# Four-layer vision kernel: dt·u·B moved to TensorE as a product with diagonal matrices, C·h to GpSimd, the scan as a pipeline of two-state units

## Chip, cores and metric

One core of one Trainium2 chip. The time is the device time of one execution in microseconds; the three runs of the kernel before have a median of 46869.22 us. All arithmetic is fp32.

## What is computed

x is [4 images, 64 x 64 pixels, 192 channels]. Four layers, each `x = x + layer(groupnorm(x))`:

- Layers 0 and 3 (state space scans over an image): project x to u (384 channels in layer 0, 192 in layer 3), depthwise 3x3 convolution and silu. Then the 4096 pixels are one sequence, taken in four orders: by rows, by columns, and both backwards. The four results are added, normalised, gated and projected back.
- Layer 1: the same kind of scan, with each image row (and each image column) as a sequence of its own of 64 pixels, forwards and backwards: four blocks with 384 channels, each with its own projections and a convolution of four taps.
- Layer 2: Toeplitz products along rows and columns. The change doesn't touch it.

The scan at the heart of layers 0, 1 and 3, for each channel and each of 16 states n:

```python
dA = jnp.exp(dt_l[..., None] * A[None])
h = dA * h + (dt_l * u_l)[..., None] * Bl[:, :, None, :]
y = jnp.sum(h * Cl[:, :, None, :], axis=-1)
```

dt has a value per channel and pixel (a softplus of a projection of rank 12); B and C have 16 values per pixel, the same for all channels. D·u is added to y.

## The kernel before

Channels lie on partitions, in NT tiles of P: 3 of 128 in layers 0 and 1, 2 of 96 in layer 3. Pixels run along the free dimension. A **job** is one chunk of 512 pixels of one image in one order: 4 images x 4 orders x 8 chunks = 128 jobs in each of the three layers.

`prepare` (line 101) makes the steps of a job: one projection of u gives 44 rows, the rank-12 part of dt, B and C (line 111). B and C go to DRAM (line 115). Per tile a second matmul and ScalarE and VectorE instructions make delta and dtu = delta·u (lines 121 to 139).

`scan` (line 143) is one job's loop over n = 0..15. For two states at a time, B and C are loaded from DRAM, broadcast over the partitions (line 159, 1 MB, 0.75 MB in layer 3). Then for each n:

1. VectorE: h = dtu·B, one product over all NT tiles (line 161, [P, NT x 512]); it is issued for n + 1 before the product with C for n.
2. ScalarE: dA = exp(A·delta), one instruction a tile (line 179 in layer 1, line 188 otherwise).
3. VectorE: the scan h = dA·h + h. In layers 0 and 3 one instruction a tile (line 191), which starts from `carry`, the state at the end of the previous chunk, which ScalarE copies out (line 194). In layer 1 one instruction over all tiles (line 184): dA holds zeros where a sequence begins.
4. VectorE: hc = h·C (line 198).
5. TensorE: y += I·hc, one matmul a tile that adds up in PSUM over n (line 200); y begins with D·u, a matmul with a diagonal matrix (line 172).

`run_jobs` (line 90) writes the order out by hand: the steps after the last job (layer 1: gate and output projection; layers 0 and 3: `add` of y to `acc`, line 311) and those that prepare the next job are spread evenly between the sixteen n of a scan. Each engine runs its own queue in that order; all DMAs are issued from SyncE's queue (SP).

In layers 0 and 3, `ss2d_input` leaves u in SBUF; a job in column order reads it through a strided view (`view`, line 300). PSUM: two one-bank buffers `mm` for projections, and two of three banks for y.

Of the kernel before, what the change touches and what calls it, by code (L numbers as in the profile page):

```python
# [7 lines left out]
F32 = mybir.dt.float32  # L8
# [5 lines left out]
B, HW, L = 4, 64, 4096  # images, their side, pixels of one  # L14
C = 192  # channels of the residual stream, as two tiles of 96 partitions
PC, KC = 96, 2
N = 16  # states per channel
R = 12  # rank of the step sizes
E = R + 2 * N
T = 512  # pixels of one chunk  # L20
NCH = L // T
ROWS = T // HW  # image rows (or columns) of one chunk
NG = 2  # states per load of the broadcast B and C
D1, PD, KD = 576, 96, 6  # channels of the Toeplitz layer, as six tiles of 96


class Kernel:
    def __init__(self, ctx, tc, ins, out):
        self.tc, self.nc, self.i, self.out = tc, tc.nc, ins, out
        nc = self.nc  # L30
        self.const = ctx.enter_context(tc.tile_pool(name="const", bufs=1))
        self.dram = ctx.enter_context(tc.tile_pool(name="dram", bufs=1, space=DRAM))
        self.bcd = ctx.enter_context(tc.tile_pool(name="bcd", bufs=4, space=DRAM))
        self.ident = self.const.tile([128, 128], F32, name="ident")
        make_identity(nc, self.ident)
        self.group = self.const.tile([PC, PC], F32, name="group")
        nc.sync.dma_start(self.group, ins["c_group"])
        # Turns each half of the partitions round.
        self.flip = self.const.tile([128, 128], F32, name="flip")
        nc.sync.dma_start(self.flip, ins["c_flip"])  # L40
        self.eps = self.const.tile([128, 1], F32, name="eps")
        nc.vector.memset(self.eps, 1e-5)
# [41 lines left out]
    # A job is one chunk: P, NT channel partitions and tiles; u(), its inputs [P, NT, T] or  # L84
    # [P, NT, ROWS, HW]; w, the weights; rev, whether it runs backwards; first, whether its state
    # starts at 0; carry, the state between chunks by n (None: each image row or column is a
    # sequence of its own, and dA holds tiles that are 0 where one begins); before, steps that
    # make u; after(y), steps that use the chunk's y, its D u included, from PSUM.

    def run_jobs(self, jobs, pools):  # L90
        """The steps before the next chunk and after the last one go between those of a scan."""
        for step in self.prepare(jobs[0], pools):
            step()
        after = []
        for job, following in zip(jobs, jobs[1:] + [None]):
            between = after + (self.prepare(following, pools) if following else [])
            after = job["after"](self.scan(job, pools, between))
        for step in after:
            step()

    def prepare(self, job, pools):
        """Steps to delta, delta u, and B and C in DRAM."""
# [4 lines left out]
        def project():  # L107
            u = job["u"]()
# [5 lines left out]
            job["bc"] = self.bcd.tile([2, N, T], F32, name="bc_dram")  # L114
            nc.sync.dma_start(job["bc"].rearrange("a n l -> (a n) l"), xd[R:E, :])
            job["delta"] = prep.tile([P, NT, T], F32, name="delta")
            job["dtu"] = prep.tile([P, NT, T], F32, name="dtu")
            job["e"] = prep.tile([P, NT, T], F32, name="e", bufs=1)

        # softplus(v) = max(v, 0) + log1p(exp(-|v|)), log1p(e) = ln(q) + (e - (q - 1)), q = 1 + e  # L120
        def step_size(t):
            dp = mm.tile([P, T], F32, name="dt_ps", tag="mm")
            nc.tensor.matmul(dp, w["dtw"][:, t * P : (t + 1) * P], job["xd"][0:R, :], start=True, stop=True)  # L123
# [10 lines left out]
        def finish():  # L134
            e, delta, dtu, u = job["e"], job["delta"], job["dtu"], job["u"]()
            nc.vector.tensor_sub(delta, delta, e)  # L136
            nc.vector.tensor_add(delta, delta, dtu)  # L137
            by_line = lambda ap: ap.rearrange("p t (a b) -> p t a b", b=HW) if len(u.shape) == 4 else ap
            nc.vector.tensor_mul(by_line(dtu), by_line(delta), u)

        return job["before"] + [project] + [lambda t=t: step_size(t) for t in range(NT)] + [log1p, finish]

    def scan(self, job, pools, between):
        nc = self.nc
        P, NT, w, rev, carry = (job[k] for k in ("P", "NT", "w", "rev", "carry"))
        delta, dtu, scratch, u = job["delta"], job["dtu"], job["bc"], job["u"]()
        work = pools["work"]
        lines = lambda ap: ap.rearrange("p (a b) -> p a b", b=HW)
        flat = lambda ap: ap.rearrange("p t l -> p (t l)")
        way = slice(None, None, -1) if rev else slice(None)  # L150
        inner = slice(0, HW - 1) if rev else slice(1, HW)
        last = 0 if rev else T - 1
        bc = {}

        def state_input(n):
            if n % NG == 0:
                bc[n // NG] = pools["bc"].tile([P, 2, NG * T], F32, name="bc")
                src = scratch[:, n : n + NG, :].rearrange("a n l -> a (n l)")
                nc.sync.dma_start(bc[n // NG], src.unsqueeze(0).broadcast_to([P, 2, NG * T]))
            h = work.tile([P, NT, T], F32, name="h")  # L160
            nc.vector.tensor_mul(h, dtu, spread(n, 0))  # L161
            return h

        def spread(n, which):
            at = (n % NG) * T
            return bc[n // NG][:, which, at : at + T].unsqueeze(1).broadcast_to([P, NT, T])

        if job.get("begin"):
            job["begin"]()
        y = pools["y"].tile([P, NT, T], F32, name="y")  # L170
        for t in range(NT):
            nc.tensor.matmul(y[:, t, :], w["D"][:, t, :], u[:, t], start=True, stop=False)  # L172
        h_next = state_input(0)
        for n in range(N):
            h = h_next
            if carry is None:
                dA = job["dA"][n % len(job["dA"])]
                for t in range(NT):
                    nc.scalar.activation(  # L179
                        lines(dA[:, t, :])[:, :, inner], lines(delta[:, t, :])[:, :, inner],  # L180
                        AF.Exp, scale=w["A"][:, t, n : n + 1],
                    )
                h_way = flat(h)[:, way]
                nc.vector.tensor_tensor_scan(h_way, flat(dA)[:, way], h_way, 0.0, ALU.mult, ALU.add)  # L184
            else:
                dA = work.tile([P, NT, T], F32, name="dA")
                for t in range(NT):
                    nc.scalar.activation(dA[:, t, :], delta[:, t, :], AF.Exp, scale=w["A"][:, t, n : n + 1])  # L188
                for t in range(NT):
                    start = 0.0 if job["first"] else carry[n][:, t : t + 1]  # L190
                    nc.vector.tensor_tensor_scan(  # L191
                        h[:, t, way], dA[:, t, way], h[:, t, way], start, ALU.mult, ALU.add
                    )
                nc.scalar.copy(carry[n], h[:, :, last])  # L194
            if n + 1 < N:
                h_next = state_input(n + 1)
            hc = work.tile([P, NT, T], F32, name="hc")
            nc.vector.tensor_mul(hc, h, spread(n, 1))  # L198
            for t in range(NT):
                nc.tensor.matmul(y[:, t, :], self.ident[:P, :P], hc[:, t, :], start=False, stop=n == N - 1)  # L200
            for step in between[len(between) * n // N : len(between) * (n + 1) // N]:
                step()
        return y

    def neg_exp(self, A):
        """A_log -> -exp(A_log), in place."""
# [4 lines left out]
    def ss2d(self, pre, x_in, x_out, P, NT, ways, bias_twice):  # L211
        tc, nc, ins = self.tc, self.nc, self.i
        DI = P * NT
        xn_d = self.image_tiles(f"{pre}xn")
        with tc.tile_pool(name=f"{pre}lay", bufs=1) as lay:
# [5 lines left out]
            D = self.load(lay, "D", ins[f"{pre}D"])  # L221
            dtb = self.load(lay, "dtb", ins[f"{pre}dt_b"])
# [7 lines left out]
            u = lay.tile([P, NT, L], F32, name="u")  # L230
            acc = lay.tile([P, NT, L], F32, name="acc")
            for b in range(B):
                self.ss2d_input(x_in[b], xn_d[b], u, P, NT, inw, cw, cb)
                self.ss2d_scan(pre, u, acc, P, NT, ways, A, D, dtb)
                self.ss2d_output(x_in[b], xn_d[b], x_out[b], acc, P, NT, inw, ow, g, be, avg)

    def ss2d_input(self, x_in, xn_d, u, P, NT, inw, cw, cb):
        """Group norm, input projection, depthwise 3x3 convolution, silu -> u."""
        tc, nc = self.tc, self.nc
        S = HW + 2  # L240
        with (
            tc.tile_pool(name="a", bufs=1) as pa,
            tc.tile_pool(name="a_small", bufs=1) as small,
# [583 lines left out]
```

## Time and profile before

| | |
|---|---|
| Runs | 46856.47, 46869.22, 46886.22 us |
| Profiled execution, span | 46860.2 us |
| Mean granted TensorE clock | 0.761 |
| DMA | 3594.65 MB, mean 77 GB/s |
| Layer 0, jobs of one image (204 to 4046 us) | 3842 us for 32 jobs |
| Layer 1, all jobs (16955 to 31620 us) | 14665 us for 128 jobs |

The profiled execution is one execution; its span runs from the first to the last instruction. In lines of groups, columns are: line of the kernel, engine, operation, tiles written and read, shapes, count, then busy time in us, mean ns of one, and idle time of the engine before them with what ended it. PE is TensorE (PEld its weight loads), DVE is VectorE, ACT ScalarE, POOL GpSimd.

### The profile page before, as it was taken

Reading aid. Unit: us, or ns where it says so; the run is one execution under the profiler, and the core shown is the slowest. Engines: PE = TensorE matmul, PEld = TensorE weight load, DVE = VectorE, ACT = ScalarE, POOL = GpSimd, SP = SyncE. Lnnn points to the kernel's source line nnn. Section 1 sums busy time; section 2 is a strip of 40 time slices with the busy share of each in tenths; the row PEclk is TensorE's granted clock in tenths of the full one; section 3 lists DMA queues with packets and bytes.
Section 4 is the critical chain, followed back from the end, with each engine's and each line's share of the span. In section 5 each row is a group of like instructions: output and inputs, shape, how many; then the busy total and the mean of one; then the engine's idle time right before and its main releaser. Section 6 shows DMA issues by size and latency. Waiting matters only on the chain. (4 is left out here: it accounts for less than half of the span.)

```text
span 46860.2 us, 220354 instructions
## 1 busy us (share of the span) xinstructions
PE 34545.4 (74%) x67176; PEld 12468.0 (27%) x67176; DVE 42630.1 (91%) x28512; ACT 18863.3 (40%) x29431; POOL 96.4 (0%) x30
## 2 busy tenths in 40 slices
PE   6666666666666667777777777777887877878778
PEld 2222222222222223333333333332652222222222
DVE  9999999899999989999999999992226999999999
ACT  3333333333333335555555555550323333333333
POOL 0000000000000000000000000000000000000000
PEclk7777777777777788888888888887997555565555
DMA  2221222222222232222222222224333222222222
GB/s 67 71 70 65 70 71 70 65 70 70 65 71 70 70 97 80 80 81 81 80 81 80 80 81 80 80 79 103 70 84 85 80 75 80 78 77 79 76 80 78
DMA packets 1162895, 3594.65 MB, mean 77 GB/s; under 512 B 229685, under 2 KB 234374, under 8 KB 1153638
## 3 DMA queue, kind: packets, MB, share of 16 engines
q1 hardware_dynamic: 1161702, 3580.55, 25.1%
q8 instruction: 528, 8.65, 0.1%
q14 instruction: 665, 5.45, 0.0%
HBM read 3353.17 MB, written 227.08 MB: 76 GB/s over the span
## 5 line engine op out<-in xcount | busy, mean ns | idle before, releaser
L200 PE MATMUL y<-hc,ident 128*128 128x512 f32 (+1 forms) x32768 | 22752.0, 854 | 9493.5 <-DVE hc L198 9492.8
L200 PEld LDWEIGHTS y<-hc,ident 128*128 128x128 f32 (+1 forms) x32768 | 7791.3, 253 | 24490.0 <-DVE hc L198 14676.2
L191 DVE TENSOR_TENSOR_SCAN h<-dA,carry,h 128x512 f32<-128x512 f32 (+1 forms) x8960 | 10904.3, 1268 | 0.0
L198 DVE TENSOR_TENSOR hc<-h,bc 128x1536 f32<-128x1536 f32 (+1 forms) x6144 | 9562.3, 1570 | 17.0 <-PE y L200 2.1
L161 DVE TENSOR_TENSOR h<-dtu,bc 128x1536 f32<-128x1536 f32 (+1 forms) x6144 | 9502.4, 1565 | 7.6 <-ACT carry L194 1.1
L194 ACT COPY carry<-h 128x3 f32<-128x3 f32 (+1 forms) x4096 | 794.2, 194 | 15450.3 <-DVE h L191 15450.2
L184 DVE TENSOR_TENSOR_SCAN h<-dA,h 128x1536 f32<-128x1536 f32 x2048 | 6757.3, 3341 | 0.0
L188 ACT ACTIVATE dA<-delta,A 128x512 f32<-128x512 f32 (+1 forms) x10240 | 6691.0, 711 | 3.1
L179 ACT ACTIVATE dA<-delta,A 128x504 f32<-128x504 f32 x6144 | 3959.4, 706 | 4961.1 <-DVE h L184 4672.5
L172 PE MATMUL y<-u,Dd 128*128 128x512 f32 (+1 forms) x2048 | 1281.5, 750 | 628.8 <-issue 601.8
L191 DVE TENSOR_TENSOR_SCAN h<-dA,h 128x512 f32<-128x512 f32 (+1 forms) x1280 | 1479.7, 1206 | 0.0
L501 PE MATMUL conv_ps<-pad,taps 128*128 128x512 f32 x3072 | 1381.8, 591 | 0.0
L132 ACT ACTIVATE delta<-delta 128x1536 f32<-128x1536 f32 (+1 forms) x384 | 515.1, 1341 | 1480.4 <-DVE e L131 1479.0
L111 PE MATMUL xd_ps<-u,xw 128*44 128x512 f32 (+1 forms) x1280 | 1023.1, 927 | 87.4 <-ACT dtu L125 87.4
L123 PE MATMUL dt_ps<-xd,dtw 12*128 12x512 f32 (+1 forms) x1280 | 897.3, 825 | 235.8 <-ACT dtu L125 208.9
L524 PE MATMUL o_ps<-z,out_w 128*96 128x512 f32 x1536 | 819.9, 692 | 331.5 <-DVE z L519 304.0
L179 ACT ACT_TABLE_LOAD x764 | 980.2, 1283 | 35.0 <-DVE delta L137 21.1
L123 PE MATMUL dt_ps<-xd,dt_w 12*128 12x512 f32 x768 | 481.4, 738 | 539.1 <-ACT xd L113 539.1
L635 DVE TENSOR_TENSOR qv<-q,v 96x512 f32<-96x512 f32 x192 | 132.0, 688 | 790.7 <-ACT v L633 790.7
L136 DVE TENSOR_TENSOR delta<-delta,e 128x1536 f32<-128x1536 f32 (+1 forms) x384 | 601.4, 1566 | 203.5 <-ACT delta L132 203.5
L448 DVE SCALAR_TENSOR_TENSOR xo<-fc_ps,fb,xr 96x512 f32<-96x512 f32 x64 | 47.8, 747 | 809.0 <-PE fc_ps L445 809.0
L501 PEld LDWEIGHTS conv_ps<-pad,taps 128*128 128x128 f32 x3072 | 578.9, 188 | 740.7 <-issue 738.3
(136 smaller groups left out, 22109.0 us busy)
## 6 DMA issues: line engine op xcount, KB each, us to landing
bc<-bc_dram SPq DMA_DIRECT2D x2048, 1024.0 KB
bc<-bc_dram SPq DMA_DIRECT2D x1024, 768.0 KB
xn<-t_xn SPq DMA_DIRECT2D x224, 384.0 KB
m_out<-o SPq DMA_DIRECT2D x256, 192.0 KB
x<-xo SPq DMA_DIRECT2D x96, 384.0 KB
x<-x SPq DMA_DIRECT2D x24, 1536.0 KB
xr<-x SPq DMA_DIRECT2D x96, 384.0 KB
mat<-t_a SPq DMA_DIRECT2D x24, 1536.0 KB
```

The costliest lines, as they stand in the source:

```text
L111: nc.tensor.matmul(ps, w["xw"][:, t, :], u[:, t], start=t == 0, stop=t == NT - 1)
L123: nc.tensor.matmul(dp, w["dtw"][:, t * P : (t + 1) * P], job["xd"][0:R, :], start=True, stop=True)
L161: nc.vector.tensor_mul(h, dtu, spread(n, 0))
L172: nc.tensor.matmul(y[:, t, :], w["D"][:, t, :], u[:, t], start=True, stop=False)
L179: nc.scalar.activation(lines(dA[:, t, :])[:, :, inner], lines(delta[:, t, :])[:, :, inner], AF.Exp, scale=w["A"][:, t, n : n + 1],)
L184: nc.vector.tensor_tensor_scan(h_way, flat(dA)[:, way], h_way, 0.0, ALU.mult, ALU.add)
L188: nc.scalar.activation(dA[:, t, :], delta[:, t, :], AF.Exp, scale=w["A"][:, t, n : n + 1])
L191: nc.vector.tensor_tensor_scan(h[:, t, way], dA[:, t, way], h[:, t, way], start, ALU.mult, ALU.add)
L198: nc.vector.tensor_mul(hc, h, spread(n, 1))
L200: nc.tensor.matmul(y[:, t, :], self.ident[:P, :P], hc[:, t, :], start=False, stop=n == N - 1)
L501: nc.tensor.matmul(ps, w["taps"][:, t, j, :], pad[:, t, :, o : o + HW], start=j == 0, stop=j == 3)
L524: nc.tensor.matmul(ps, w["out_w"][:, t, m * PC : (m + 1) * PC], job["z"][:, t, :], start=t == 0, stop=t == NT - 1,)
```

## The change

The work is cut into **units**: two states (a pair p) of one channel tile t, so 8 x NT units a job (24 in layers 0 and 1, 16 in layer 3). `run_jobs` is now a pipeline over the units of all jobs: in iteration i it issues `feed` of unit i + 2, `scan` of unit i, `collect` of unit i - 1, for a job's last pair `add` of unit i - 2, and then the steps of the neighbouring jobs that are due.

- `turn(t)` transposes dtu on TensorE to dtuT (pixels on partitions), `turn_b` does the same with B. Eight DRAM tiles `diags`, filled with zeros once, receive B for four states on the diagonals of four 128 x 128 blocks (512 pieces of 16 bytes), and each is loaded as a whole (1 MB) into `diag`.
- `feed`: for each block of 128 pixels one matmul dtuT^T · diag with 256 columns (pixel and state, the state running faster) gives dtu·B of two states in PSUM (`b`, two buffers of two banks). In layers 0 and 3 the columns go to PSUM in that order and the scan reads every second word. In layer 1 the output's access pattern puts the two states 256 words apart, so that a scan reads 1024 words in order.
- `scan`: VectorE's scan takes dA from SBUF and b from PSUM; hc = h·C is a GpSimd product over 1024 elements. `collect`: two matmuls with I into y, which is now one bank a tile.
- C alone is loaded in broadcast (`fetch`, 0.5 MB a pair); `fetch` of pair p + 2 is issued in the feed of pair p, the first two in `turn_b`.
- In layers 0 and 3, u is written to DRAM in row and in column order and each job loads its chunk; D·u of all four orders is put into `acc` at the first order's `add` (a sum of the four D), without a matmul. In layer 1 D·u stays a matmul.
- `mm` has one buffer instead of two; `dtu` one instead of two.

The core of the diff (the removed bodies, the weights' reordering to B, C, dt and the new pools' arguments are left out):

```diff
+        self.diags = [self.dram.tile([128, NB, 128, 4], F32, name=f"diag{j}") for j in range(8)]
...
     def run_jobs(self, jobs, pools):
...
+        units = [(k, p, t) for k, job in enumerate(jobs) for p in range(N // 2) for t in range(job["NT"])]
+        last = N // 2 - 1
+        per = len(units) // len(jobs)
+        steps = []
+        for i in range(-AHEAD, len(units) + 2):
+            if 0 <= i + AHEAD < len(units):
+                k, p, t = units[i + AHEAD]
+                self.feed(jobs[k], p, t, pools)
+            if 0 <= i < len(units):
+                k, p, t = units[i]
+                self.scan(jobs[k], p, t, pools)
+            if 0 <= i - 1 < len(units):
+                k, p, t = units[i - 1]
+                self.collect(jobs[k], p, t, pools)
+            if 0 <= i - 2 < len(units):
+                k, p, t = units[i - 2]
+                if p == last:
+                    jobs[k]["add"](t)
+            if 0 <= i < len(units):
+                k, q = divmod(i, per)
+                if q == 2:
+                    steps = (jobs[k - 1]["after"]() if k else []) + (
+                        self.prepare(jobs[k + 1], pools) if k + 1 < len(jobs) else []
+                    )
+                    given, count = 0, len(steps)
+                if q >= 2:
+                    due = min(count, -(-count * (q - 1) // (per - 2 - AHEAD)))
+                    for step in steps[given:due]:
+                        step()
+                    given = due
...
+        def turn_b():
+            ps = mm.tile([128, NB, N], F32, name="b_ps", tag="mm")
+            for k in range(NB):
+                nc.tensor.transpose(ps[:, k, :], job["xd"][0:N, k * 128 : (k + 1) * 128], self.ident[:N, :N])
+            job["bt"] = prep.tile([128, NB, N], F32, name="bt")
+            nc.scalar.copy(job["bt"], ps)
+            job["cbc"], job["diag"] = {}, {}
+            for p in range(2):
+                self.fetch(job, p, pools)
...
+        def turn(t):
+            ps = mm.tile([128, NB, P], F32, name="dtu_ps", tag="mm")
+            for k in range(NB):
+                nc.tensor.transpose(
+                    ps[:, k, :], job["dtu"][:, t, k * 128 : (k + 1) * 128], self.ident[:P, :P]
+                )
+            nc.scalar.copy(job["dtuT"][:, t], ps)
+
+        each = lambda f: [lambda t=t: f(t) for t in range(NT)]
+        return job["before"] + [project] + each(step_size) + [log1p, finish] + each(turn) + [turn_b]
+
+    def fetch(self, job, p, pools):
+
+        nc, P = self.nc, job["P"]
+        c = job["cbc"][p] = pools["c"].tile([P, 2 * T], F32, name="c")
+        src = job["c"][4 * p : 4 * p + 4, :].rearrange("a l -> (a l)")
+        nc.sync.dma_start(c, src.unsqueeze(0).broadcast_to([P, 2 * T]))
+        if p % 2 == 0:
+            self.turns += 1
+            d = self.diags[self.turns % len(self.diags)]
+            row = NB * 128 * 4
+            to = bass.AP(d.tensor, d.offset, [[row + 4, 128], [128 * 4, NB], [1, 4]])
+            nc.sync.dma_start(to, job["bt"][:, :, 2 * p : 2 * p + 4])
+            job["diag"][p // 2] = self.load(pools["diag"], "diag", d)
+
+    def feed(self, job, p, t, pools):
...
+        if t == 0 and p + 2 < N // 2:
+            self.fetch(job, p + 2, pools)
+        b = pools["b"].tile([P, 2 * T], F32, name="b")
+        diag = job["diag"][p // 2]
+        lines = job["carry"] is None
+        for k in range(NB):
+            if lines:
+                to = b.rearrange("p (h n l) -> p h l n", h=2, n=2)
+                at = k % 2 * 128
+                to = to[:, k // 2, at : at + 128, :]
+            else:
+                to = b[:, k * 256 : (k + 1) * 256].rearrange("p (l n) -> p l n", n=2)
+            at = p % 2 * 2
+            nc.tensor.matmul(to, job["dtuT"][:, t, k, :], diag[:, k, :, at : at + 2], start=True, stop=True)
...
+    def scan(self, job, p, t, pools):
...
+        b, dA = job["fed"].pop((p, t))
+        h = pools["work"].tile([P, 2 * T], F32, name="h", bufs=3)
+        if carry is None:
+            nc.vector.tensor_tensor_scan(h[:, way], dA[:, way], b[:, way], 0.0, ALU.mult, ALU.add)
+        else:
+            by_n = b.rearrange("p (l n) -> p n l", n=2)
+            hn = h.rearrange("p (n l) -> p n l", n=2)
+            for n in range(2):
+                start = 0.0 if job["first"] else carry[p, t][:, n : n + 1]
+                nc.vector.tensor_tensor_scan(
+                    hn[:, n, way], dA[:, n, way], by_n[:, n, way], start, ALU.mult, ALU.add
+                )
+            nc.scalar.copy(carry[p, t], hn[:, :, 0 if rev else T - 1])
+        hc = pools["work"].tile([P, 2 * T], F32, name="hc")
+        nc.gpsimd.tensor_mul(hc, h, job["cbc"][p])
+        job["done"][p, t] = hc
...
+        for n in range(2):
+            if job["carry"] is None:
+                of = hc.rearrange("p (h n l) -> p h n l", h=2, n=2)[:, :, n, :]
             else:
...
+                of = hc[:, n * T : (n + 1) * T]
+            nc.tensor.matmul(
+                y, self.ident[:P, :P], of, start=p == 0 and n == 0 and "D" not in job["w"],
+                stop=p == N // 2 - 1 and n == 1,
+            )
...
+                by_col = pu.tile([P, HW, HW], F32, name="by_col", bufs=1)
+                nc.scalar.activation(
+                    by_col.rearrange("p b a -> p a b"), o, AF.Silu, bias=cb[:, t : t + 1]
+                )
+                nc.scalar.activation(o, o, AF.Silu, bias=cb[:, t : t + 1])
+                for to, of in zip(u_d, (o, by_col)):
+                    nc.sync.dma_start(to[:, t, :], of.rearrange("p a b -> p (a b)"))
...
+            tc.tile_pool(name="s_mm", bufs=1, space=PSUM) as mm,
+            tc.tile_pool(name="s_b", bufs=2, space=PSUM) as bp,
+            tc.tile_pool(name="s_y", bufs=1, space=PSUM) as yp,
...
+                    def load(job=job, col=col, c=c):
+                        job["u"] = self.load(prep, "u", u_d[col][:, :, c * T : (c + 1) * T])
```

## Prediction

> **What bounds the kernel now.** I read the page's busy shares first, then one steady window of each scan layer, then the groups of instructions by shape, then PE's order of time. DVE is the engine without slack; GpSimd does nothing:
>
> ```profile
> PE 34545.4 (74%) x67176; PEld 12468.0 (27%) x67176; DVE 42630.1 (91%) x28512; ACT 18863.3 (40%) x29431; POOL 96.4 (0%) x30
> ```
>
> One window of 1000 us each in layers 0, 1 and 3 (columns: window, length, busy PE, PEld, DVE, ACT, POOL, granted PE clock, DMA share, GB/s):
>
> ```profile
> 5000.00:6000.00 1000.00, 676.95 (x940) 223.76 (x938) 988.76 (x705) 360.47 (x627) 0.00 (x0) 0.77 0.21 70
> 20000.00:21000.00 1000.00, 776.02 (x1512) 308.54 (x1511) 989.54 (x476) 534.75 (x712) 5.63 (x4) 0.88 0.25 82
> 38800.00:39800.00 1000.00, 792.99 (x948) 209.11 (x947) 998.10 (x869) 394.21 (x727) 0.00 (x0) 0.56 0.29 80
> ```
>
> DVE is busy 99% in all three. The same windows for line 161, of which a job (one chunk of 512 pixels) has 16:
>
> ```profile
> 5000.00:6000.00 1000.00, 230.07 (x133) 0.77 0.21 70
> 20000.00:21000.00 1000.00, 239.32 (x140) 0.88 0.25 82
> 38800.00:39800.00 1000.00, 239.43 (x200) 0.56 0.29 80
> ```
>
> So a job takes 16/133, 16/140 and 16/200 ms: 120, 114 and 80 us in layers 0, 1, 3, 128 jobs each. These 40.2 ms are the sum's base; the other 6.7 ms of the span (inputs, outputs, layer 2) I leave alone but for 0.3 ms below. DVE's groups:
>
> ```profile
> L198 DVE TENSOR_TENSOR hc<-h,bc 128x1536 f32<-128x1536 f32 x4096 | 7075.9, 1748 | 0.4
> L161 DVE TENSOR_TENSOR h<-dtu,bc 128x1536 f32<-128x1536 f32 x4096 | 7052.6, 1745 | 5.2
> L184 DVE TENSOR_TENSOR_SCAN h<-dA,h 128x1536 f32<-128x1536 f32 x2048 | 6757.3, 3341 | 0.0
> L191 DVE TENSOR_TENSOR_SCAN h<-dA,carry,h 128x512 f32<-128x512 f32 x5376 | 6510.5, 1269 | 0.0
> ```
>
> The two products (9.5 + 9.6 ms over all shapes) are what leaves DVE; the scans stay. PE's real pace comes from starts, not from durations (the page says that ends are modelled). Timeline of PE and PEld:
>
> ```profile
> 33051.05 14.21 PE L703 MATMUL o_ps<-flip,yt 128*96 128x128 f32 x128 [1.11 <-ACT yt L699]
> ...
> 32043.55 3.62 PE L445 MATMUL fc_ps<-h,fw 96*96 96x512 f32 x8
> ...
> 32053.87 7.04 PE L445 MATMUL fc_ps<-v,fw 96*96 96x512 f32 x8
> ...
> 40004.70 0.28 PEld L200 LDWEIGHTS y<-hc,ident 96*96 96x96 f32 x1 [0.57 <-issue]
> 40005.55 0.28 PEld L200 LDWEIGHTS y<-hc,ident 96*96 96x96 f32 x1 [0.57 <-issue]
> ```
>
> A matmul of the program is two instructions here (32768 for 16384 calls of line 200). At full clock one of 512 columns starts every 0.43 us (h, the next group began at 32047.00), one of 128 every 0.110; in the throttled state it is 0.85. And v, the same matmul read from a column-order view (stride 64 words), takes 0.86 at full clock (the next group began at 32060.72): an access pattern alone doubled it.
>
> [...]
>
> **The change part by part.** A unit is two states of one channel tile: 24 units a job in layers 0 and 1, 16 in layer 3.
>
> DVE loses lines 161 and 198. Left in layer 0: 48 scans at 1.18 us (3.63 us for a run of three, 3.54 from start to start in the timeline) = 57, preparation 4 x 1.7 = 7, three adds 3: 67 us a job. Layer 1: 24 scans of 1024 = two thirds of 3.27 (457.63/140) = 2.2 us, 53, with the rest 62. Layer 3: 38 + 5 + 3 = 46. A PSUM operand in the scan isn't in this trace; at 2.3 ns an element the scan is not limited by reading, so I take no change, and +10% as the far end (73, 68, 50): still not the bound.
>
> GpSimd gets one product of 1024 elements a unit. [...] Hidden below PE; [...]
>
> ACT keeps its exponentials and gains three copies of dtu transposed and one of B (0.6 us each). Layer 1's 535 busy of 1000 become about 600 of 1000 at the old pace: hidden. `carry` stays (0.2 us).
>
> PE keeps two y matmuls a unit (4 instructions of 512: 4 x 0.43 = 1.72 us) and gains four b matmuls of 256 columns, 8 instructions. Between 0.110 and 0.43 that is 0.216 us each: 1.73. Sum 3.44 us a unit against DVE's 2.4: PE becomes the bound. Per job at full clock:
> - Layer 0: 24 x 3.44 = 82.7; x and dt projections 12 x 0.43 = 5.1 (the D matmul goes into the add); 12 transposes at 0.11 and four tiny ones 1.6. 89.4 us.
> - Layer 1: 82.7 + 78 x 0.43 (39 matmuls of projections, convolution, D, output) = 33.5 + 1.6: 117.8 us. That is more than the 114 of today before any stall.
> - Layer 3: 16 x 3.44 = 55.1 + 3.4 + 0.9 = 59.4 us.
>
> The diagonals' read takes two neighbouring words[...]. Ends: 0.216 and 0.43. The write: in layers 0 and 3 contiguous. In layer 1 the two states are sent 256 words apart, so successive columns alternate. [...] its size I take from the nearest row, v against h: twice, 0.43. Ends 0.216 and 0.43; chosen 0.43[...]. Cost: 192 x 0.216 = 41.5 us a job, layer 1 becomes 159.
>
> New wait: `turn_b` is the last step before a new job and issues the first c load, the diagonal's scattered DRAM write and the 1 MB load behind it on SP's queue; the first b matmul of the next job waits for that, one unit later in layers 0 and 3, at once in layer 1. Queued behind it on PE: the y products of the last two units, then DVE and GpSimd run dry. A write and its dependent load, at the start of the kernel:
>
> ```profile
> 171.99 0.31 SPq L115 DMA_DIRECT2D bc_dram<-xd  x1
> ...
> 173.60 0.91 SPq L159 DMA_DIRECT2D bc<-bc_dram  x2
> ```
>
> 1.6 us for the write; 512 pieces of 16 bytes may be slower: 1.6 to 5, taken 2.5. The load: 1.05 MB at 70 GB/s / 0.21 = 333 GB/s is 3.1, plus the same 1.6. With the ACT copy and issue (0.8): 8 us. Less one unit (3.4): about 5 us open in layers 0 and 3, 8 in layer 1. [...] Ends: 0 (if loads come early) and 15. Later diagonals are asked for six units ahead (four in layer 3, 14 us): hidden; without that cover 8 us twice a job. SP's own work: about 19 issues of 0.36 us a job against 9, with four write waits: 14 us of 80 or more. Bytes per job are about the same.
>
> `log1p` and `finish` hold DVE some 5 us each while PE has one unit in stock; 4 us a job in layer 0, 1.5 in layer 3, 1 in layer 1 (an estimate from these durations). The single `mm` buffer costs about 1 us where two steps share a unit: in that estimate.
>
> Sum per job: layer 0 89.4 + 4 + 7.5 = 101 (-19); layer 1 159 + 1 + 10.5 = 170.5 (+56.5); layer 3 59.4 + 1.5 + 7.5 = 68.5 (-11.5). Times 128: -2.4, +7.2, -1.5. u by way of DRAM lengthens the start of each of the 8 images (two Silu passes of 3.7, 2 MB of writes, a load, the diagonal chain: about 30 us), and eight 1 MB zero writes delay the start by some 25 us: +0.3 ms. Altogether +3.6 on 46.86 (the profiled execution; its span is 9 us below the median shown, which changes nothing): **50.4 ms**.
>
> **The rivals.** *The alternating write is free* (the other side): [...] For it: [...] the read side's doubling need not carry over. Layer 1 is then 117.8 + 11 = 129 (+1.9 ms), the total -2.4 + 1.9 - 1.5 + 0.3 = -1.7: **45.2 ms**. It decides at 0.285 us a b instruction in layer 1 (24576 of them cost 1.7 ms per 0.069). *Pairs in the read are slow too*: 41.5 more in layer 0, 27.6 in layer 3: +8.8, **59.2 ms**. [...] *The diagonal chain takes 15 us and the clock stays low*: +8 us a job in three layers, **53.4 ms**.
>
> **How the numbers follow.** Alternating write slow 0.48; free 0.32; pairs slow 0.08; GpSimd 0.06; chain 0.06. The likeliest has its own range 48.5 to 52.5. The free write reaches from 43.9 (no bubbles) to 46.9. Leaving out the slow pairs and the tails, 44.3 to 53.0. A measurement tells 0.2% from no change. Faster 0.30 (nearly all of the second case), same 0.03, slower 0.67.
>
> **What would show it.** Right: PE near 95% and DVE near 60% in layers 0 and 3; b matmuls starting 0.22 us apart in layers 0 and 3 and 0.43 in layer 1; one PE wait of 5 to 8 us per job on the diagonal's load[...]. Wrong: b at 0.22 in layer 1; DVE or POOL at 99%; layer 1's jobs near 129 us.

## The result and the profile after

Before and after, run on the same chip: 46877.72 us (median of 4, 46856.47 to 46886.46) and 46926.68 us (median of 4, 46921.5 to 46933.6). The ratio is 1.0011, with a 95% interval of 0.9996 to 1.0025: **no measurable change**, where 50.4 ms was forecast.

The profiled execution after has a span of 46919.7 us and a mean granted clock of 0.945 (before: 46860.2 and 0.761). The busy shares have changed places. PE, 74% before, is the busiest engine, VectorE fell from 91% to 55%, and GpSimd works:

```profile
PE 41500.0 (88%) x137064; PEld 23014.5 (49%) x137064; DVE 26034.8 (55%) x17814; ACT 20137.6 (43%) x32128; POOL 20138.3 (43%) x8231
```

One window of 1000 us each in layers 0, 1 and 3 (columns as in the prediction's windows):

```profile
5000.00:6000.00 1000.00, 916.45 (x2978) 549.11 (x2977) 661.07 (x519) 445.84 (x835) 560.43 (x227) 0.97 0.28 86
20000.00:21000.00 1000.00, 909.60 (x2742) 512.18 (x2741) 484.79 (x226) 473.93 (x625) 422.89 (x174) 0.96 0.22 66
40000.00:41000.00 1000.00, 920.97 (x3033) 462.68 (x3032) 693.09 (x543) 463.48 (x874) 552.17 (x229) 0.99 0.36 111
```

PE stands at 91 or 92% where VectorE stood at 99%. GpSimd does one product a unit, so the count in its column is that of units: 24/227, 24/174 and 16/229 ms are 106, 138 and 70 us a job. From one transposition of B to the next the median job after is 106.1, 139.5 and 69.8 us; later jobs are measured in the same way.

For the sum, the stretches count in which scans run, from an image's first scan to its last (in layer 1 from the first of all to the last), read from VectorE's instructions in both traces:

| Layer | Before, us a job | Predicted | After, us a job | Before, ms | After, ms | Difference |
|---|---|---|---|---|---|---|
| 0 | 120.4 | 101 | 105.5 | 15.41 | 13.51 | -1.90 ms |
| 1 | 115.5 | 170.5 | 138.8 | 14.78 | 17.77 | +2.99 ms |
| 3 | 80.3 | 68.5 | 69.3 | 10.28 | 8.87 | -1.40 ms |

(Layer 1's last scan before starts at 31756 us; the row of the table of the kernel before, which ends at 31620, lacks the last job's end.) These are -0.31 ms. What lies outside the stretches grew by 0.37: from an image's last scan to the next one's first it is 381 us instead of 335 in layer 0 and 294 instead of 257 in layer 3, and the first scan of all starts at 257.0 instead of 194.9 us. Together that is the +0.06 ms of the spans. So the change moves the time a great deal, and it comes out even because layer 1 and the starts give back what layers 0 and 3 gain. That the two sides cancel this closely is chance.

The groups (line, engine, operation, tiles, count, then busy us, mean ns of one, and idle time before them with its cause):

```profile
L277 POOL TENSOR_TENSOR hc<-h,c 128x1024 f32<-128x1024 f32 (+1 forms) x8192 | 20036.5, 2449 | 21843.0 <-PE y L296 14022.5
L237 PE MATMUL b<-diag,dtuT 128*128 128x256 f32 (+1 forms) x65536 | 17206.0, 406 | 2313.8 <-DMA diag<-diag 1396.8
L272 DVE TENSOR_TENSOR_SCAN h<-dA,carry,b 128x512 f32<-128x512 f32 (+1 forms) x8960 | 10926.3, 1263 | 5426.7 <-PE b L237 5060.5
L266 DVE TENSOR_TENSOR_SCAN h<-dA,b 128x1024 f32<-128x1024 f32 x3072 | 6999.0, 2283 | 8599.3 <-PE b L237 8537.2
```

VectorE and GpSimd wait for PE: the scans for b, the next product for y to free its buffer. What ends most of PE's idle time before b is one DMA, the load of a job's first diagonal. How fast b runs is read from starts, not from the modelled durations. Layer 1, timeline of PE (start, length, line, tiles, count):

```profile
22015.99 1.98 PE L237 MATMUL b<-diag,dtuT 128*128 128x256 f32 x8
22017.81 1.88 PE L296 MATMUL y<-hc,ident 128*128 128x512 f32 x4
22019.52 1.88 PE L607 MATMUL in_ps<-xn,in_w 96*128 96x512 f32 x4
```

Eight b instructions take 22017.81 - 22015.99 = 1.82 us, 0.227 each, in the layer whose write alternates; the median pitch is 0.227 us in layers 0 and 3 too. The forecast had 0.43 here. The job's start, also in layer 1, on PE and on SyncE's queue:

```profile
21975.70 0.42 PE L166 MATMUL b_ps<-ident,xd 16*128 16x16 f32 x4
...
21984.15 1.02 PE L646 MATMUL o_ps<-z,out_w 128*96 128x512 f32 x2
21990.79 8.49 PE L237 MATMUL b<-diag,dtuT 128*128 128x256 f32 x24 [5.62 <-DMA diag<-diag]
```

```profile
21977.35 2.02 SPq L217 DMA_DIRECT2D diag<-bt  x4
21979.99 3.66 SPq L58 DMA_DIRECT2D diag<-diag  x2
21983.75 0.38 SPq L211 DMA_DIRECT2D c<-c_dram  x1
21986.36 0.32 SPq L58 DMA_DIRECT2D diag<-diag  x1
```

From B's transposition to the first b 15.1 us pass; PE has other work for the first 9.5 and stands still for the last 5.6. Of the 15.1, 1.7 us go to the transposition, ScalarE's copy and the issue, 2.6 to the DRAM write until its load is issued, and 10.8 to that load. The queue doesn't run as the program is written: the writes of all four diagonals of the job come one after the other, and three of the four loads (1 MB each) start within 7 us. In all 217 jobs of layers 0 and 1 between 500 and 14000 and between 16000 and 30000 us the four writes come before the first load, and three loads start within 8 us; from the first load's issue to the first b it is a median of 10.4 to 10.5 us. In layer 3 the diagonals mostly come two at a time, and where PE waits for one it is 6.9 us. No run here separates the loads, so that they hold each other up is not shown.

Then 24 b instructions take 8.49 us, 0.35 each instead of 0.227. The first 14 start 0.43 us apart, and the granted clock in that stretch (the column before the last two) is 0.50; the ten behind them are back at 0.227:

```profile
21990.80:21996.70 5.90, 5.90 (x14) 4.71 (x15) 1.99 (x1) 0.00 (x0) 0.00 (x0) 0.50 0.83 349
```

### The profile page after: what moved, and what is told of

Same layout as the page of the kernel before. It is cut to its first block, busy times and chain, and to the rows that moved or that the text cites. A ratio compares the mean times of both kernels' runs of the same rounds, so it can differ in the third digit from the quotient of the medians.

```text
span 46919.7 us, 374033 instructions
## 1 busy us (share of the span) xinstructions
PE 41500.0 (88%) x137064; PEld 23014.5 (49%) x137064; DVE 26034.8 (55%) x17814; ACT 20137.6 (43%) x32128; POOL 20138.3 (43%) x8231
## 4 chain that ended last, share of the span: by engine, by line
PE 63%; DVE 17%; DMA 11%; ACT 4%; issue 4%; POOL 0%; SPq 0%; DVEq 0%; ACTq 0%; POOLq 0%
PE b L237 25%; PE y L296 18%; DMA diag<-diag 7%; DVE h L272 6%; DVE h L266 3%; PE conv_ps L623 3%; DMA diag<-bt 2%; PE xd_ps L148 2%; PE dt_ps L176 2%; PE fc_ps L565 2%; DVE dtu L193 2%; DVE delta L191 2%; DVE delta L192 2%; PE z_ps L607 1%; PE in_ps L607 1%
## 5 line engine op out<-in xcount | busy, mean ns | idle before, releaser
L277 POOL TENSOR_TENSOR hc<-h,c 128x1024 f32<-128x1024 f32 (+1 forms) x8192 | 20036.5, 2449 | 21843.0 <-PE y L296 14022.5
L237 PE MATMUL b<-diag,dtuT 128*128 128x256 f32 (+1 forms) x65536 | 17206.0, 406 | 2313.8 <-DMA diag<-diag 1396.8
L237 PEld LDWEIGHTS b<-diag,dtuT 128*128 128x128 f32 (+1 forms) x65536 | 12148.8, 190 | 8659.6 <-issue 4301.7
L296 PE MATMUL y<-hc,ident 128*128 128x512 f32 (+1 forms) x32768 | 15513.8, 596 | 375.5 <-POOL hc L277 375.3
L272 DVE TENSOR_TENSOR_SCAN h<-dA,carry,b 128x512 f32<-128x512 f32 (+1 forms) x8960 | 10926.3, 1263 | 5426.7 <-PE b L237 5060.5
L266 DVE TENSOR_TENSOR_SCAN h<-dA,b 128x1024 f32<-128x1024 f32 x3072 | 6999.0, 2283 | 8599.3 <-PE b L237 8537.2
L296 PEld LDWEIGHTS y<-hc,ident 128*128 128x128 f32 (+1 forms) x32768 | 5905.4, 183 | 5956.0 <-issue 4297.8
L275 ACT COPY carry<-h 128x2 f32<-128x2 f32 (+1 forms) x5120 | 986.0, 193 | 12387.8 <-DVE h L272 12374.5
L272 DVE TENSOR_TENSOR_SCAN h<-dA,b 128x512 f32<-128x512 f32 (+1 forms) x1280 | 1484.8, 1204 | 857.9 <-PE b L237 850.4
L186 DVE SCALAR_TENSOR_TENSOR e<-delta,e 128x1536 f32<-128x1536 f32 (+1 forms) x384 | 1013.9, 2640 | 620.1 <-ACT delta L185 620.1
```

What stands on the lines that cost most here:

```text
L237: nc.tensor.matmul(to, job["dtuT"][:, t, k, :], diag[:, k, :, at : at + 2], start=True, stop=True)
L266: nc.vector.tensor_tensor_scan(h[:, way], dA[:, way], b[:, way], 0.0, ALU.mult, ALU.add)
L272: nc.vector.tensor_tensor_scan(hn[:, n, way], dA[:, n, way], by_n[:, n, way], start, ALU.mult, ALU.add)
L277: nc.gpsimd.tensor_mul(hc, h, job["cbc"][p])
L296: nc.tensor.matmul(y, self.ident[:P, :P], of, start=p == 0 and n == 0 and "D" not in job["w"], stop=p == N // 2 - 1 and n == 1,)
```

## Experiments

Ratios are to the kernel before as measured beside each of them, 46852 to 46883 us. Code that is left out is marked by `...`.

**1. The write in layer 1, straightened.**

```diff
-            if lines:
-                to = b.rearrange("p (h n l) -> p h l n", h=2, n=2)
-                at = k % 2 * 128
-                to = to[:, k // 2, at : at + 128, :]
-            else:
-                to = b[:, k * 256 : (k + 1) * 256].rearrange("p (l n) -> p l n", n=2)
+            to = b[:, k * 256 : (k + 1) * 256].rearrange("p (l n) -> p l n", n=2)
...
-            nc.vector.tensor_tensor_scan(h[:, way], dA[:, way], b[:, way], 0.0, ALU.mult, ALU.add)
+            by_n = b.rearrange("p (l n) -> p n l", n=2)
+            hn, dn = (ap.rearrange("p (n l) -> p n l", n=2) for ap in (h, dA))
+            for n in range(2):
+                nc.vector.tensor_tensor_scan(
+                    hn[:, n, way], dn[:, n, way], by_n[:, n, way], 0.0, ALU.mult, ALU.add
+                )
...
```

What is left out lays C, dA and y's operand out in the same order. So layer 1's one scan of 1024 becomes two of 512 as well.

> The changed kernel, with layer 1's b written to PSUM as in layers 0 and 3: columns in a row instead of 256 words apart (so its scan becomes two of 512 instead of one of 1024, and C is loaded in the plain order). Theory of the prediction: the alternating write costs; without it b goes from the pace it has to a faster one, up to 41.5 us a job, 5.3 ms: 41.6 ms. Rival: the write is free, b starts 0.227 us after b in both: within 0.3 ms of 46.9.

Measured: 46704.97 us, ratio 0.9966 (0.9954 to 0.9979), 0.2 ms below the changed kernel. Layer 1's timeline:

```profile
22015.48 1.97 PE L227 MATMUL b<-diag,dtuT 128*128 128x256 f32 x8
22017.30 1.88 PE L288 MATMUL y<-hc,ident 128*128 128x512 f32 x4
```

Again 1.82 us for eight, and the median pitch in layer 1 is 0.227 us in both kernels. The alternating write costs nothing here, and the prediction's main step is refuted. The 0.2 ms is not b's pace: layer 1's job went from 139.5 to some 137.5 us, and what changed there are PE's waits. In the 12 ms from 18000 us on, the one for dtu fell from 5.2 to 0.9 us a job, and the one for the scan, which frees a buffer of b, rose from 0.6 to 3.3.

**2. The diagonals asked for earlier.**

```diff
-        return job["before"] + [project] + each(step_size) + [log1p, finish] + each(turn) + [turn_b]
+        return job["before"] + [project] + each(step_size) + [log1p, finish, turn_b] + each(turn)
```

> The changed kernel, with turn_b (and the C loads, the diagonals' write and their load that it issues) put ahead of the three turns instead of behind them. Theory 1: PE is the bound, and the chain of B's transposition, DRAM write and 1 MB load stands open at every job's start. The trace has 1397 us of PE idle time behind that load, and I make the slow clock after the job changes another 970 us: 46.9 - 2.0 = 44.9 ms (44.3 to 45.6), and the wait on diag all but gone. Rival: the load only happens to come last; the pipeline from b by way of the scan to y is empty at a job's start anyway and the wait goes over to the turned dtu: 46.5 to 47.0 ms.

Measured: 43907.57 us, ratio 0.9371 (0.9357 to 0.9385), 3.0 ms below the changed kernel. PE's wait for the diagonals (total us, times, longest) was 1396.8 us in 356 waits before this edit; the window in layer 1 shows PE at 96% instead of 91:

```profile
PE b L237 <- DMA diag<-diag: 121.5, 86, 3.9
```

```profile
20000.00:21000.00 1000.00, 962.59 (x2974) 547.25 (x2974) 520.72 (x244) 510.80 (x677) 454.99 (x188) 0.98 0.25 74
```

Jobs are 96.2, 128.7 and 66.9 us: the open chain cost 10, 11 and 3 us a job in layers 0, 1 and 3. It is more than the 2.0 ms that I had read from PE's waits and the clock. The profile shows what makes up the 3.0:

```profile
PE 40554.2 (92%) x137064; PEld 22780.1 (52%) x137064; DVE 26005.3 (59%) x17814; ACT 20129.2 (46%) x32128; POOL 20095.2 (46%) x8231
```

PE's busy time for the same 137064 instructions fell from 41500.0 us by 0.95 ms, which agrees with the 970 us that I had put on the slow clock. Its time without work, span less busy, fell from 5419.7 to 3380.1 us, by 2.04 ms: 1.28 of that is the wait for the diagonals, and the rest came from elsewhere (y's wait for GpSimd fell from 375 to 10 us, the one for dtu from 866 to 655). Theory 1 holds and is undersized; the rival falls. One line moved makes the changed kernel 6% faster than the one before.

**3. What PE still waits for in layer 1.** With the diagonals early, PE waits ahead of the transposition of dtu, then runs eight b at about half speed (20178.00 - 20174.58 = 3.42 us against 1.82, 0.43 each, the pace that the clock of 0.50 gave at the job's start above):

```profile
20167.15 1.88 PE L296 MATMUL y<-hc,ident 128*128 128x512 f32 x4
20173.70 1.09 PE L198 MATMUL dtu_ps<-ident,dtu 128*128 128x128 f32 x4 [4.68 <-DVE dtu L193]
20174.58 3.62 PE L237 MATMUL b<-diag,dtuT 128*128 128x256 f32 x8
20178.00 2.17 PE L296 MATMUL y<-hc,ident 128*128 128x512 f32 x4
```

First try: other PE work in between. To the kernel of experiment 2, the three gate projections of layer 1 are moved behind `turn_b`:

```diff
-        return job["before"] + [project] + each(step_size) + [log1p, finish, turn_b] + each(turn)
+        return job["before"] + [project] + each(step_size) + [log1p, finish, turn_b] + job.get("gates", []) + each(turn)
...
-            before=([weights] if begin else []) + [load] + each(input_of) + each(convolve) + each(gate),
+            before=([weights] if begin else []) + [load] + each(input_of) + each(convolve),
+            gates=each(gate),
```

> The changed kernel with turn_b early, and layer 1's three gate projections put between turn_b and the turns, so that PE has work while VectorE finishes dtu. In the run with turn_b early PE still waited 4.8 us a job in layer 1 ahead of the transposition of dtu. Theory 1 (VectorE's preparation is what PE waits for): that goes, 0.6 ms: 43.3 ms. Rival (the wait moves to the next step in line): 43.8 to 44.0 ms.

Measured: 44057.38 us, ratio 0.9397 (0.9381 to 0.9412), no gain. The rival holds: the wait has moved to the single `mm` buffer. Waits in the 2 ms from 20000 us on (total us, times, longest; some 15 jobs):

```profile
PEld z_ps L607 <- ACT z L630: 72.3, 15, 4.8
...
PE z_ps L607 <- ACT z L630: 59.9, 15, 4.0
```

In the job at 20200 us ScalarE's silu, which empties `mm`, is queued behind exponentials that wait 5.66 us for a scan, and this scan comes behind products of the preparation on VectorE, one of which takes 3.79 us. So the cover didn't help, because PE and ScalarE both came to wait for VectorE.

Second try, again from the kernel of experiment 2: keep GpSimd from holding up VectorE in layer 1, by putting h·C of this layer alone on VectorE.

```diff
-        nc.gpsimd.tensor_mul(hc, h, job["cbc"][p])
+        (nc.vector if carry is None else nc.gpsimd).tensor_mul(hc, h, job["cbc"][p])
```

> The changed kernel with turn_b early, and h*C on VectorE in layer 1 alone. Theory 1 (PE waits 4.8 us a job in layer 1 for dtu because GpSimd's product lengthens VectorE's preparation): that wait falls to about 0.8 us, as in the run with h*C on VectorE throughout: 43.9 - 0.5 = 43.4 ms. Rival (VectorE, which then has 90 of 128 us to do, is late elsewhere and gives it back): 43.8 ms or more.

Measured: 43406.97 us, ratio 0.9265 (0.925 to 0.9281), 0.5 ms below experiment 2. Layer 1's job is 124.7 us instead of 128.7, and the preparation's last product (18000 to 30000 us; first the kernel of experiment 2, then this one) shows why:

```profile
L193 DVE TENSOR_TENSOR dtu<-delta,u 128x1536 f32<-128x1536 f32 x93 | 346.1, 3722 | 3.1
```

```profile
L193 DVE TENSOR_TENSOR dtu<-delta,u 128x1536 f32<-128x1536 f32 x95 | 166.4, 1752 | 0.0
```

3.72 us beside GpSimd, 1.75 alone. PE's wait for dtu in the same stretches went from 4.7 to 0.6 us a job:

```profile
PE dtu_ps L198 <- DVE dtu L193: 433.7, 93, 4.7
```

```profile
PE dtu_ps L198 <- DVE dtu L193: 60.2, 95, 0.6
```

Theory 1 holds.

**4. Each part of the change alone.** Only TensorE's product, h·C back on VectorE everywhere:

```diff
-        nc.gpsimd.tensor_mul(hc, h, job["cbc"][p])
+        nc.vector.tensor_mul(hc, h, job["cbc"][p])
```

> The other part alone: the changed kernel with h*C on VectorE instead of GpSimd. Theory 1: PE is the bound, and GpSimd's product is hidden; VectorE has 2.4 + 1.17 us a unit against 4.4: the time is that of the changed kernel, or some tenths of a ms better, since hc comes 1.3 us earlier and the preparation's products go back from 2640 to 1754 ns: 46.3 to 46.9 ms. Rival 1: y waits for GpSimd in every unit, so the change loses what GpSimd was given: under 45.5 ms. Rival 2: the product delays the next scan and so the freeing of b's two buffers: over 47.5 ms.

Measured: 47255.08 us, ratio 1.0086 (1.0071 to 1.0101), 0.3 ms above the changed kernel. The total hides two signs: jobs are 108.6, 136.1 and 73.8 us, so GpSimd is worth 2.5 and 4 us a job in layers 0 and 3, and costs 3.4 us in layer 1. In this run VectorE is busy 86, 66 and 84% in the windows of layers 0, 1 and 3, so it is nearer its limit where GpSimd pays; that this is the reason was not tested. No theory had it whole.

Only GpSimd's product, in the kernel before:

```diff
-            nc.vector.tensor_mul(hc, h, spread(n, 1))
+            nc.gpsimd.tensor_mul(hc, h, spread(n, 1))
```

> One part of the change alone: the kernel before, with its product h*C (line 198) on GpSimd instead of VectorE; dtu*B stays on VectorE, the scan reads SBUF. Theory 1 (the two engines don't hold each other up): VectorE's jobs lose 28, 28 and 18.5 us in layers 0, 1 and 3, GpSimd has 16 products of about 3.6 us: 46.9 - 9.5 = 37.4 ms. Theory 2 (every VectorE instruction with two SBUF inputs stands still while a GpSimd product runs): the 28 us gained come back as 58 us of waiting, 10 ms lost: 57 ms. In between (VectorE at half pace during a GpSimd product, as the preparation's products in the changed kernel suggest, 2640 instead of 1754 ns): about 46.9 ms.

Measured: 55653.2 us, ratio 1.1877 (1.1859 to 1.1894): 19% slower, near theory 2. Some of it was VectorE standing still for a buffer of h; the same with three buffers of h (`bufs=3` at line 160):

> The kernel before with h*C on GpSimd, as in the earlier run of this part alone, and three buffers for h instead of two. In that run VectorE stood still for 7.1 ms until GpSimd had done with an h, and its own instructions got longer: 132, 110 and 85 us of busy time a job in layers 0, 1 and 3, where 92, 86 and 62 were left. Theory 1 (the longer instructions are the loss): the standing still goes, the jobs come to those 132, 110 and 85 us against 120, 114 and 80: 46.9 + 1.6 = 48.5 ms, still slower than before. Rival (the two buffers made the loss): 92, 86 and 62 us, below 40 ms.

Measured: 55058.79 us, ratio 1.1752 (1.1735 to 1.177). The standing still is gone (VectorE is busy 90% of the span), but line 161 has gone from 2166 to 3142 ns: taking away the wait for a buffer made the instructions longer, and my 48.5 ms was far too low. Both look like one and the same wait for GpSimd. Groups of this kernel:

```profile
L198 POOL TENSOR_TENSOR hc<-h,bc 128x1536 f32<-128x1536 f32 (+1 forms) x6144 | 26590.7, 4334 | 23390.9 <-DVE h L191 15453.8
L161 DVE TENSOR_TENSOR h<-dtu,bc 128x1536 f32<-128x1536 f32 (+1 forms) x6144 | 19080.2, 3142 | 124.4 <-DMA bc<-bc_dram 62.0
L191 DVE TENSOR_TENSOR_SCAN h<-dA,carry,h 128x512 f32<-128x512 f32 (+1 forms) x8960 | 14905.5, 1722 | 0.0
```

Line 161 takes 3142 ns, twice the 1565 of the kernel before; the scan from SBUF 1722 against 1268. Timelines of VectorE and GpSimd in layer 0:

```profile
2003.85 1.73 DVE L161 TENSOR_TENSOR h<-dtu,bc 128x1536 f32<-128x1536 f32 x1
2005.50 4.98 DVE L131 SCALAR_TENSOR_TENSOR e<-delta,e 128x1536 f32<-128x1536 f32 x1
2010.40 3.63 DVE L191 TENSOR_TENSOR_SCAN h<-dA,carry,h 128x512 f32<-128x512 f32 x3
```

```profile
2004.10 4.76 POOL L198 TENSOR_TENSOR hc<-h,bc 128x1536 f32<-128x1536 f32 x1 [2.43 <-DVE h L191]
```

Line 131 starts at 2005.50, GpSimd's product ends at 2008.86, and line 131 ends 1.6 us after that, where alone it takes 1.75: it did next to nothing while GpSimd ran. This is no single case. Of line 161's 4096 products of 1536 elements, 2430 start while a GpSimd product runs. They take 4.97 us (the median), and 2421 of them end 1.6 us after it; the 638 that meet none take 1.75. The three scans at 2010.40, with GpSimd idle, take their old 3.63 us.

In the changed kernel the scan reads b from PSUM and takes 1263 ns (line 272 above); with h·C on VectorE it is 1262. So the two parts belong together: **where GpSimd's product pays, it does so because TensorE's product takes the product from SBUF off VectorE and puts one of the scan's inputs into PSUM.** Without it, GpSimd's product makes line 161 9.6 ms longer in all (19080.2 against 9502.4 us) and the scans of line 191 4.0 ms (14905.5 against 10904.3). The two halves of TensorE's part were not tried one by one.

**5. Is PE the bound?** The kernel of experiment 2 without the second state of each pair in y:

```diff
-        for n in range(2):
+        for n in range(1):
             if job["carry"] is None:
                 of = hc.rearrange("p (h n l) -> p h n l", h=2, n=2)[:, :, n, :]
...
-                stop=p == N // 2 - 1 and n == 1,
+                stop=p == N // 2 - 1,
```

> The changed kernel with turn_b early, and with the second state of each pair left out of y (the sum over states has 8 terms instead of 16; everything else is computed as before). Theory 1 (PE's own work sets the pace): 24, 24 and 16 times 0.86 us less a job, 20.6, 20.6 and 13.8 us, 7.0 ms: 36.9 ms. Rival (the loop b, scan, h*C, y with two buffers of each sets it: PE only waits longer): less than half of it, over 40.4 ms.

Measured: 37694.66 us, ratio 0.8041 (0.8029 to 0.8053), 6.2 ms below experiment 2 of the 7.0 of theory 1. Jobs are 80.3, 109.2 and 54.0 us, 15.8, 19.5 and 12.9 less, where 20.6, 20.6 and 13.8 were taken out of PE. PE's work sets the pace; layer 0 gives only three quarters of it, and PE's waits there for the scan and for GpSimd grew from 2.6 to 5.3 us a job (the 2 ms from 500 us on). The same in a form that computes everything: the gates late, and D·u of layer 1 on VectorE instead of three matmuls (`Dcol` holds D, and y begins with the first state).

```diff
...
-            nc.vector.tensor_mul(job["z"][:, t, :], job["y"][t], job["z"][:, t, :])
+            u, D, z = job["u"][:, t, :], w["Dcol"][:, t : t + 1], job["z"][:, t, :]
+            nc.vector.scalar_tensor_tensor(u, u, D, job["y"][t], ALU.mult, ALU.add)
+            nc.vector.tensor_mul(z, u, z)
...
```

> As the run before with the gates late, and D*u of layer 1 added by VectorE in the gate (one instruction a tile more) instead of three PE matmuls. Theory 1 (PE is the bound to the last matmul): 6 instructions of 0.43 us less a job, 2.6 us, 0.33 ms below the run with the gates late: 43.0 ms. Rival (the job's end waits for VectorE, which now has one more instruction there): equal to it or above.

Measured: 43629.61 us, ratio 0.9306 (0.9293 to 0.932), 0.43 ms below the run with the gates late where 0.33 was expected. Theory 1 holds.

**6. The better of both.** Layer 1 as before (with `run_jobs`, `prepare`, `scan` and `mamba_job` of the kernel before under other names), layers 0 and 3 as after, with `turn_b` early:

```diff
-            self.run_jobs(jobs, pools)
+            self.run_old(jobs, pools)
...
```

> Layer 1 as in the kernel before (VectorE makes both products, one scan over three tiles), layers 0 and 3 as in the changed kernel with turn_b ahead of the turns. If the layers add up (128 jobs of 114.6 us in place of the 128.5 of the run with turn_b early): 43.9 - 1.8 = 42.1 ms, which beats both kernels. Rival: layer 1's old jobs are slower beside the new DRAM layout or lose their own start, 42.8 ms or more.

Measured: **42278.32 us**, ratio 0.9018 (0.9004 to 0.9031), 9.8% faster than the kernel before. Adding up the layers had given 42.1. Layer 1, where PE has 39 matmuls a job besides y, b and the transpositions, is the one to leave alone.

## Why the prediction was wrong

**The bound moves from VectorE to PE: right.** The matmuls at full clock, by the median pitches in the trace and the counts of a job, are 92.1, 120.4 and 61.3 us a job; forecast 89.4, 117.8 and 59.4. Experiment 5 confirms that PE's work sets the pace.

**"chosen 0.43": this step failed.** It is the 41.5 us a job that made layer 1 170.5 us, 5.3 ms and with them the sign of the forecast. An fp32 write whose columns alternate 256 words apart ran at 0.227 us, like the contiguous one, and straightening it changed nothing in b (experiment 1). That such a write is slow no trace had shown: the nearest row that I took, v against h, was a read from SBUF, and nothing had made it evidence for a write.

**The rival that held, "the alternating write is free", gave 45.2 ms, and that is 1.7 too low.** Its own terms, by layer: -1.90 ms instead of -2.4 in layer 0, +2.99 instead of +1.9 in layer 1, -1.40 instead of -1.5 in layer 3, and between the stretches +0.37 instead of +0.3. The starts were right, then, and layers 1 and 0 make the difference. The terms behind it:

- *The diagonals' chain.* Forecast 7.5, 10.5 and 7.5 us a job: waits of 5, 8 and 5, the rest for a slow clock after them, which no trace had then shown; in the job above the slow clock took 14 x 0.2 = 2.8 us. Experiment 2 gave 10, 11 and 3 in all. That layer 1 fits is luck: the chain was 15.1 us and not 8, and PE had 9.5 us of other work where the forecast had none. The chain's write was right (2.6 us for 2.5); the load was mis-sized, 10.8 us instead of 4.7. "Later diagonals are asked for six units ahead" is not what the queue did (the job's start above). The rival "the diagonal chain takes 15 us" had the length, and not the price. The sign named for it, "one PE wait of 5 to 8 us per job on the diagonal's load", came true in layer 1 (5.5 us, the median wait) and nearly in layer 0 (4.5); in layer 3 it is 0.8.
- *The preparation on VectorE.* Forecast 1 us a job in layer 1, "an estimate from these durations" of the kernel before. PE's wait for dtu was 5.2 us, and 4.0 us of the job went away when GpSimd left VectorE alone (experiment 3). That GpSimd makes these products longer (the last of them 3.72 us beside it, 1.75 alone), and so delays the new transposition of dtu on PE, the prediction put at nothing.
- *The pitches.* b takes 0.227 us for 0.216: 192 x 0.011 = 2.1 us a job in layers 0 and 1. A matmul of the dt projection takes 0.525 for 0.43, six of them 0.6 us. PE's wait for the scan, which frees b's buffers, is another 2.6 us a job in layer 0 after experiment 2. These were not tested singly.

**GpSimd hidden: right for the total, wrong by layer.** 2.45 us a product, 43% busy, never the bound; what the forecast took for a product was not shown by any trace. The scan took no longer from PSUM than from SBUF before (1263 ns against 1268), as forecast, and beside GpSimd no longer than without it (1263 against 1262 ns; in layer 1 2283 against 2282). A product with two SBUF inputs did: 4.97 us for 1.75 where it starts beside a GpSimd product (experiment 4).

**The pair read runs at full speed: right to 5%.** 0.227 us in layers 0 and 3 against the forecast 0.216, which was taken between 0.110 for 128 columns and 0.43 for 512 and, for this read, shown by no trace; PE's cost per unit is 1.82 + 1.71 = 3.53 us against 3.44.

## What to carry to other kernels

When work moves to another engine, add up that engine's whole load in each stage, at the pitch of its own starts: the same edit gained 15 us a job in layer 0, where PE has some 7 us of work besides y and b, and lost 23 in layer 1, where 39 further matmuls make it some 36. A slowdown that would double a stage's new instructions, and that only a row of another kind suggests (a read here, for a write), should be a rival of equal weight and not the forecast's base. After such a move look first at the new dependent chain at the stage's start: here moving one step ahead by three places was worth 6%.

## What the hardware showed unexpectedly

- An fp32 matmul that writes PSUM with columns alternating 256 words apart ran as fast as a contiguous one: 0.227 us per 256 columns. Other types were not measured.
- A VectorE product of 1536 fp32 elements a partition from SBUF took 3.72 us on average instead of 1.75 beside GpSimd products, and one that started during a GpSimd product hardly advanced until that had ended (it ended 1.6 us later in 2421 of 2430 cases). A scan with one input in PSUM wasn't touched (1263 ns beside GpSimd's products, 1262 without them).
- After 5.62 us without work PE's first 14 b instructions started 0.43 us apart instead of 0.227, at a granted clock of 0.50. After 4.7 us without work (experiment 3) eight took 3.42 us instead of 1.82: 1.6 us on top of the wait.
- In the kernel before, the matmul that reads v (stride 64 words) starts every 0.858 us at a granted clock of 1.0 and of 0.5 alike (medians of 359 and 101 starts), where its neighbour h goes from 0.429 to 0.853. So the slow read lost nothing more at the lower clock.
